# A decoder kernel: silus ahead of the second gates, projection at the tenth scan state, and the halves of a rotation ahead of its sum of squares

## The chip, the cores and the metric

The kernel runs on one core of a Trainium2 chip. TensorE (PE) multiplies matrices into PSUM, VectorE (DVE) and ScalarE (ACT) do the elementwise work and reductions, GpSimd (POOL) does elementwise work on SBUF alone, and SyncE (SP) issues transfers. Each engine takes its instructions in order; semaphores hold one until another engine's result is there or a buffer is free. The metric is the device time of one execution in microseconds (us), as the median of several runs.

## The reference

Two decoder layers work on x of shape (4, 512, 128), all in float32. Layer 0 is a selective state-space block, a cross attention and a mixture of experts; layer 1 is a banded attention, a cross attention, and a small transformer of two sublayers with local attention. The change touches the first and the last of these. Cut to what matters:

```python
# layer 0: selective scan, d_inner = 256, 16 states
x_part, z = split(rmsnorm(x) @ in_proj.T)
u = silu(causal_conv(x_part) + conv_b)
dt, Bm, Cm = split(u @ x_proj_w.T)
delta = softplus(dt @ dt_proj_w.T + dt_proj_b)
h[t] = exp(delta[t] * A) * h[t-1] + delta[t] * Bm[t] * u[t]   # for each of 16 states
y[t] = sum over states of h[t] * Cm[t], plus u[t] * D
out = (y * silu(z)) @ out_proj_w.T + x
```

```python
# layer 1, local attention: 8 heads of 64, windows of 64, twice
q, k, v = split(shift_token(x) @ wqkv)
q = q / clip(norm(q), 1e-12) * q_scale      # k likewise
q = q * cos * scale + rotate_half(q) * sin * scale   # k with 1 / scale
o = softmax over the own and the preceding window, times v
x = x + o @ wo;  x = x + feed_forward(layernorm(shift_token(x)))   # gated by gelu
```

## The kernel before, in words

Two stages matter. In both, the order of the instructions on every engine is written out by hand (`manual_schedule`): each helper issues its instructions when it is called, and each engine keeps that order.

**The scan** (pool "m2ps"). It steps through 4 batches of 16 states, `steps[k] = (b, n)`. One state holds two chunks of 128 channels side by side in tiles of 128x1024. Per state, ACT makes the decays `dA` (`decay`, L438, three states ahead), PE spreads the rows of B and C over the partitions (`rows`: pb and pc, two states ahead; ACT copies pc to cb, L433), DVE multiplies pb by du and scans (`scan`, L443 and L446), POOL multiplies h by cb (L451), and PE adds h to y (`collect`). pb has two PSUM buffers; pc has one, y one of two banks, h three buffers in SBUF. Beside each batch runs the preparation of the next (the table `ahead`, by state n): convolution, `gates_next` at n = 4 and 5 (PE product into a bank, ACT copy into sz, and at n = 5 the silus), `double_next` at 6 (product of u, two ACT copies), `steps_next` at 7 and 8, `parts` at 9, `corrected` and `reduced` at 10, `logarithms` and `deltas` at 11, `deltas` and `products` at 12 and 13. The preceding batch is finished beside it too: `gated` at n = 1, `projected` at 11 (16 matmuls into a bank po), `summed` at 12 (DVE reads po, L479, then the statistics, with `ve` at L179 and a POOL power), `normed4` at 14. A list `aside` gives one step of the weights' preparation for the cross attention (`blocks`, `g_part`, `v_part`) at n = 9, 10, 13 and 14; four steps each fall to batches 0, 1 and 2, the rest to n = 0 to 7 of batch 3. All of these products (gates, double, steps, projected, aside) share one PSUM bank, tag "po": a new one waits until the one before has been read for the last time.

**The local attention** (pool "la"). It goes through 32 row tiles i (two sublayers of four batches of four), each in two halves p with four heads, `g = 2 i + p`. For one g, the loop issues `scores(g+1)` (PE psc, DVE row maxima nm), `weights(g)` (PE transposes ptp, ACT copy pT), `exponentials(g+1)` (ACT), `values(g-1)` (PE pa, DVE rc and at), and around them, from the table `around`, the preparation of tiles ahead: `project_qk` of tile i+3 with `squares` (PE pqk, one PSUM buffer of two banks; ACT squares into sq, L1460), at p = 1 `rotated_a`, `norms` and `rotated_b` of tile i+3, and `turn_k`, `turn_q` of tile i+1 (PE ptk and ptq), `project_v`, `turn_out` and `output` (PE po, DVE xa, L1589). These PE results rotate through three PSUM buffers of tag "pt". The table `feed` spreads the feed-forward network over the tiles of the following batch: its gates (`ff_gates`) take pqk's buffer for two of their three products, in the tiles i = 7, 11, .. 27.

The rotation of one tile is: `rotated_a`, DVE multiplies pqk by the cosine table into ta (L1473); `norms`, DVE sums sq by head into ss (L1466) and bounds it from below (L1467); `halves`, DVE multiplies the swapped halves of pqk by the sine table into tb (L1480, two instructions, the last readers of pqk); `halves_added`, POOL adds tb to ta (L1486); `lengths`, POOL raises ss to the power -0.5 into rn (L157); `scaled`, POOL multiplies ta by rn (L1494). sq and tb share one buffer, so halves come behind the sum and the next squares behind POOL's addition. The first three tiles are prepared beside the preceding stage by the table `first`, with the calls in the order norms, rotated_a, halves, halves_added, and lengths and scaled later.

Of the kernel before, what the change touches and what calls it, by code (L numbers as in the profile page):

```python
# [11 lines left out]
F32 = mybir.dt.float32  # L12
BF16 = mybir.dt.bfloat16
I32 = mybir.dt.int32
AF = mybir.ActivationFunctionType
ALU = mybir.AluOpType
# [3 lines left out]
P = 128  # L20
# [37 lines left out]
def decoder_kernel(ctx: ExitStack, tc: tile.TileContext, a: dict):  # L58
    nc = tc.nc
    V, S, G, TE = nc.vector, nc.scalar, nc.gpsimd, nc.tensor  # L60


    cp = ctx.enter_context(tc.tile_pool(name="const", bufs=1))
# [44 lines left out]
    G.memset(cminus, -1.0)  # L108
    eps = cp.tile([P, 1], F32, tag="eps", name="eps")
    G.memset(eps, 1e-5)  # L110


    hm16 = cp.tile([P, 16], F32, tag="hm16", name="hm16")
# [123 lines left out]
    with ExitStack() as ph:  # L237
# [8 lines left out]
        u = bp.tile([P, 2, B, T], F32, tag="u", name="u")  # L246
        sz = bp.tile([P, 2, B, T], F32, tag="sz", name="sz")
# [31 lines left out]
        def unit(b):  # L279
            xns[b] = fp.tile([P, NJ, D], F32, tag="e", name="xn")  # L280
            for j in range(NJ):
                S.activation(xns[b][:, j, :], x0[:, b * NJ + j, :], AF.Identity, scale=inv[:, b, j:j + 1])
# [12 lines left out]
        def gates(b, c, pi):  # L295
            mm(pi, w_in[:, (2 + c) * P:(3 + c) * P], xnp[:, 3:])
# [64 lines left out]
        with tc.tile_pool(name="m1ps", bufs=1, space=PSUM) as ps, tc.manual_schedule():  # L361
# [9 lines left out]
            pi = ps.tile([P, T], F32, tag="pi1", name="pi")  # L371
# [5 lines left out]
            pi = ps.tile([P, T], F32, tag="pi0", name="pi")  # L377
# [36 lines left out]
        with tc.tile_pool(name="m2", bufs=3) as t2, \  # L414
# [9 lines left out]
            def rows(k):  # L424

                b, n = steps[k]
                pbs[k] = ps.tile([P, 2, T], F32, tag="pb", name="pb", bufs=2)
                for c in range(2):
                    mm(pbs[k][:, c, :], sel[:, n, :], stk[:, b, :])
                pc = ps.tile([P, T], F32, tag="pc", name="pc")  # L430
                mm(pc, sel[:, NST + n, :], stk[:, b, :])
                cbs[k] = t2.tile([P, T], F32, tag="cb", name="cb")
                S.copy(cbs[k], pc)  # L433

            def decay(k):
                b, n = steps[k]
                for c in range(2) if k else (1, 0):
                    S.activation(dAs[k % 4][:, c, c:T], delta[b % 2][:, c, c:T], AF.Exp,  # L438
                                 scale=negA[:, c * NST + n:c * NST + n + 1])

            def scan(k):
                pb = pbs.pop(k)
                V.tensor_tensor(pb, du[steps[k][0] % 2], pb, ALU.mult)  # L443
                h = hcs[k] = t2.tile([P, 2, T], F32, tag="h", name="h")
                cs = [slice(0, 2)] if k + 1 < len(steps) else [slice(0, 1), slice(1, 2)]
                V.tensor_tensor_scan(h.rearrange("p c t -> p (c t)"), dAs[k % 4].rearrange("p c t -> p (c t)"),  # L446
                                     pb.rearrange("p c t -> p (c t)"), 0.0, ALU.mult, ALU.add)
                cb = cbs.pop(k)
                for c in cs:
                    n = c.stop - c.start  # L450
                    G.tensor_tensor(h[:, c], h[:, c], cb.unsqueeze(1).to_broadcast([P, n, T]), ALU.mult)  # L451

            def collect(k):
                b, n = steps[k]
                if n == 0:
                    ys[b] = ps.tile([P, 2, T], F32, tag="y", name="y")
                hc = hcs.pop(k)
                for c in range(2):
                    mm(ys[b][:, c, :], ident, hc[:, c, :], start=n == 0, stop=n == NST - 1)

            def gated(b):
                y = ys.pop(b)
                ygs[b] = t2.tile([P, 2, T], F32, tag="yg", name="yg", bufs=1)
                for c in range(2):
                    V.scalar_tensor_tensor(ygs[b][:, c, :], u[:, c, b, :], vcol("Dp", c), y[:, c, :],
                                           ALU.mult, ALU.add)
                    (V if b == B - 1 else G).tensor_tensor(ygs[b][:, c, :], ygs[b][:, c, :], sz[:, c, b, :], ALU.mult)
# [71 lines left out]
            def bank():  # L539
                return ps.tile([P, T], F32, tag="po", name="pi")  # L540


            def turn_next(b):
                by_features(b, bank().rearrange("p (j t) -> p j t", t=P))
# [8 lines left out]
            def gates_next(b, c):  # L553
                pi = bank()
                gates(b, c, pi)
                S.copy(sz[:, c, b, :], pi)
                if c:
                    for t, i in ((u, b), (sz, b)) + ((sz, 0),) * (b == 1):
                        S.activation(t[:, :, i, :], t[:, :, i, :], AF.Silu)

            def double_next(b):
                double(b, bank()[0:104])
# [11 lines left out]
            with tc.manual_schedule():  # L574
                for k in range(3):
                    decay(k)
                for k in range(2):
                    rows(k)
                unit(1)
                turn_next(1)  # L580
                n_ = len(steps)
                for k in range(n_):
                    scan(k)
                    b, n = steps[k]
                    if k + 3 < n_:
                        decay(k + 3)
                    if k + 2 < n_:
                        rows(k + 2)
                    if n == 1 and b:
                        gated(b - 1)  # L590
                    if k:
                        collect(k - 1)
                    if b + 1 < B:
                        for f, *c in ahead.get(n, []):
                            f(b + 1, *c)
                    if n > 13 and b + 2 < B:
                        {14: unit, 15: turn_next}[n](b + 2)
                    if b and n in (11, 12, 14):
                        {11: projected, 12: summed, 14: normed4}[n](b - 1)
                    if b == B - 1 and n in (12, 13, 15):  # L600
                        {12: first_norm, 13: first_unit, 15: first_turn}[n]()
                    if aside and (n in (9, 10, 13, 14) or b == B - 1 and n < 11):
                        f, of = aside.pop(0)
                        f(of)
                assert not aside
                collect(n_ - 1)
                gated(B - 1)
                for f in (projected, summed, normed4):
                    f(B - 1)
# [372 lines left out]
    with tc.tile_pool(name="xa", bufs=3) as t1:  # L982
# [129 lines left out]
        for k in range(NT + 3):  # L1112
            for half, tile_ in enumerate((tile_a, tile_b)):
                with tc.manual_schedule():
# [3 lines left out]
                    n = 2 * k + half - 25  # L1118
# [300 lines left out]
    with tc.tile_pool(name="la_b", bufs=2) as bp, tc.tile_pool(name="la_t", bufs=2) as t1, \  # L1419
# [14 lines left out]
        hTs, pqks, tas, tbs, rns, sss, qTs, pes, pTs, ats, aTs = ({} for _ in range(11))  # L1434
# [28 lines left out]
        def norms(i):  # L1463

            ss = sm.tile([P, 16], F32, tag="ss16", name="ss16")
            V.tensor_reduce(ss, sss.pop(i).rearrange("p w h d -> p (w h) d"), AX.X, ALU.add)  # L1466
            V.tensor_scalar_max(ss, ss, 1e-24)  # L1467
            sss[i] = ss

        def rotated_a(i):  # L1470
# [3 lines left out]

        def halves(i):
            src = pqks.pop(i).rearrange("p w (h d) -> p w h d", d=64)
            tb = tbs[i] = t1.tile([P, 2, 8, 64], F32, tag="sq", name="tb", bufs=1)
            for hf in range(2):
                lo = slice(32 * hf, 32 * hf + 32)
                V.tensor_tensor(  # L1480
                    tb[:, :, :, lo], src[:, :, :, 32 - 32 * hf:64 - 32 * hf],
                    tabs[i // NT][:, i % NJ, 1, :, lo].unsqueeze(2).to_broadcast([P, 2, 8, 32]), ALU.mult)
# [11 lines left out]
            G.tensor_tensor(ta, ta, rns.pop(i).unsqueeze(2).to_broadcast([P, 16, 64]), ALU.mult)  # L1494

        def rotated_b(i):
            for f in (halves, halves_added, lengths, scaled):
                f(i)

        def turn_q(i):  # L1500
# [291 lines left out]
        def x_norm(b):  # L1792
            normal(x5[:, b * NJ:(b + 1) * NJ, :], *mvs.pop(("x", b)))


        first = {9: [(shift, 0)], 10: [(project_qk, 0), (squares, 0)],
                 11: [(norms, 0), (rotated_a, 0), (halves, 0), (halves_added, 0)],
                 12: [(project_qk, 1), (squares, 1), (lengths, 0)],
                 13: [(project_v, 0), (norms, 1), (rotated_a, 1), (halves, 1), (scaled, 0)],
                 14: [(halves_added, 1), (project_qk, 2), (squares, 2)], 15: [(lengths, 1), (turn_k, 0), (turn_q, 0)],  # L1800
                 16: [(project_v, 1), (norms, 2), (rotated_a, 2), (halves, 2), (scaled, 1)],
                 17: [(halves_added, 2)], 18: [(lengths, 2), (scores, 0)], 19: [(scaled, 2), (exponentials, 0)]}


        around = [[[], [(turn_k, 1), (turn_q, 1)], [(project_qk, 3), (squares, 3)]],
                  [[(turn_out, -1), (rotated_a, 3)], [(norms, 3), (rotated_b, 3)], [(project_v, 2), (output, -1)]]]

        feed = {(0, 0): [[], [], [(ff_hidden, 2, 0)]], (0, 1): [[], [(ff_hidden, 2, 1)], []],
                (1, 0): [[(ff_shift, 1)], [(ff_hidden, 2, 2)], []],
# [14 lines left out]
        with tc.manual_schedule():  # L1824
# [25 lines left out]
            for g in range(last):  # L1850
                i, p = divmod(g, 2)
# [183 lines left out]
```

## Time and profile before

| what | value |
|---|---|
| median of 3 runs | 1233.97 us (1232.23 to 1235.54) |
| the profiled execution: its own time | 1233.73 us |
| its span | 1231.7 us |
| granted TensorE clock, mean | 0.957 |
| busy, PE / DVE / ACT / POOL | 88 / 73 / 59 / 52% of the span |
| the scan | about 36 to 310 us |
| local attention with its prologue | about 805 us to the end |

The span is the time from the first to the last instruction of the profiled execution; its own time holds 2.0 us more. A line of a timeline gives the start (us), the duration (us), the engine, the line of the kernel, the operation, what it writes and reads with shapes, and in brackets the idle time of the engine ahead of it and what ended that. A line of waits gives the engine and line that waited, what it waited for, and the total, the number and the longest of these waits. "PEld" is TensorE's loading of weights; ptq and other names are tiles, without their buffer numbers.

### The profile page before, as it was taken

To read this page: it belongs to the slowest core of one execution; us is meant where nothing else is said; L and a number is where in the kernel's file an instruction comes from. 1 tells how busy PE (TensorE), PEld (TensorE's weight loads), DVE (VectorE), ACT (ScalarE), POOL (GpSimd) and SP (SyncE) were. 2 spreads that over 40 slices of the span, in tenths; PEclk is the share of its full clock that TensorE was granted. 3 is DMA by queue.
4 is the path that set the end of the run, shared out by engine and by line. 5 is a ranking of instruction groups with operands and counts; after the bars stand their busy time and mean duration, and the time that the engine had idled before them with its cause. 6 is when DMAs were issued, how large, how long until landed. Compare 5 with 4: busy or idle time off the path is not lost.

```text
span 1231.7 us, 22149 instructions
## 1 busy us (share of the span) xinstructions
PE 1081.4 (88%) x8377; PEld 698.5 (57%) x8377; DVE 895.8 (73%) x1691; ACT 731.2 (59%) x1629; POOL 644.7 (52%) x554
## 2 busy tenths in 40 slices
PE   5879879787778889989999998787999999999995
PEld 2324333443456679966666665455666566666564
DVE  5878888898668274867867676787777676676753
ACT  5696867764364454546566665246665765766762
POOL 5458586776454432644201111367786576576641
PEclk9799989898799899999999999899999999999998
DMA  9000000000400342300000000000110110011100
GB/s 280 1 0 1 0 1 1 0 1 0 154 1 14 137 154 76 85 27 25 2 2 2 2 2 2 0 9 19 32 28 18 28 27 18 22 24 28 27 20 28
DMA packets 38739, 39.96 MB, mean 32 GB/s; under 512 B 7544, under 2 KB 29833, under 8 KB 38153
## 3 DMA queue, kind: packets, MB, share of 16 engines
q1 hardware_dynamic: 36041, 32.73, 9.2%
q0 software_dynamic: 2048, 4.20, 1.2%
q10 hardware_dynamic: 544, 1.62, 0.5%
q8 instruction: 66, 1.08, 0.4%
q14 instruction: 40, 0.33, 0.1%
HBM read 20.80 MB, written 9.18 MB: 24 GB/s over the span
## 4 chain that ended last, share of the span: by engine, by line
PE 46%; DVE 18%; ACT 4%; issue 2%; POOL 2%; DMA 1%; DVEq 0%; ACTq 0%; POOLq 0%; SPq 0%
PE psc L189 9%; PE pa L189 4%; PE pqk L189 4%; PE ptp L1287 4%; PE po L189 3%; PE pff L189 3%; PE phg L189 3%; PE pog L189 3%; DVE tb L1480 2%; PE pv L189 2%; DVE ss L1466 2%; DVE ta L1473 2%; PE pof L189 2%; PE pq L189 1%; DMA hn<-xa 1%
## 5 line engine op out<-in xcount | busy, mean ns | idle before, releaser
L451 POOL TENSOR_TENSOR h<-h,cb 128x1024 f32<-128x1024 f32 (+1 forms) x65 | 151.8, 2337 | 72.0 <-DVE h L446 59.8
L157 POOL TENSOR_TENSOR rs<-ve,cneg 128x1 f32<-128x1 f32 (+2 forms) x74 | 56.1, 758 | 210.9 <-DVE ve L166 175.7
L446 DVE TENSOR_TENSOR_SCAN h<-dA,pb 128x1024 f32<-128x1024 f32 x64 | 146.3, 2286 | 21.7 <-PE y L189 7.4
L1277 ACT ACTIVATE pe<-psc,nm 128x256 f32<-128x256 f32 (+1 forms) x256 | 93.4, 448 | 69.7 <-DVE nm L1270 68.9
L189 PE MATMUL y<-h,ident 128*128 128x512 f32 x256 | 128.9, 628 | 6.1 <-POOL h L451 5.4
L1486 POOL TENSOR_TENSOR ta<-ta,tb 128x1024 f32<-128x1024 f32 x32 | 75.4, 2356 | 102.5 <-DVE rc L1570 56.2
L1270 DVE TENSOR_REDUCE nm<-psc 128x4 f32<-128x1024 f32 (+1 forms) x64 | 69.8, 1090 | 43.1 <-PE psc L189 37.9
L157 POOL TENSOR_TENSOR rn<-ss,cneg 128x16 f32<-128x16 f32 x32 | 93.0, 2906 | 0.0
L1540 DVE TENSOR_REDUCE nm<-psc 128x4 f32<-128x512 f32 x64 | 44.0, 687 | 63.8 <-PE psc L189 62.0
L438 ACT ACTIVATE dA<-delta,negA 128x511 f32<-128x511 f32 (+1 forms) x128 | 85.3, 715 | 6.3 <-POOL delta L352 4.4
L189 PEld LDWEIGHTS y<-h,ident 128*128 128x128 f32 x256 | 49.7, 198 | 67.5 <-issue 47.2
L940 ACT ACTIVATE hTg<-phg,bias 128x128 f32<-128x128 f32 x184 | 52.3, 368 | 46.6 <-PE phg L189 45.0
L443 DVE TENSOR_TENSOR pb<-du,pb 128x1024 f32<-128x1024 f32 x64 | 77.5, 1211 | 2.4 <-POOL du L355 1.5
L1549 ACT ACTIVATE pe<-psc,nm 128x128 f32<-128x128 f32 x256 | 73.6, 380 | 5.0 <-DVE nm L1540 4.9
L189 PE MATMUL pqk<-f_qkv,hT 128*128 128x512 f32 x128 | 65.0, 631 | 4.1 <-DVE tb L1480 4.1
L1287 PE MATMUL ptp<-ident,pe 128*128 128x128 f32 x448 | 64.9, 282 | 4.0 <-ACT pT L1289 2.0
L189 PE MATMUL psc<-kb,qk 64*128 64x256 f32 (+1 forms) x512 | 66.4, 378 | 0.0
L189 PE MATMUL pb<-stk,sel 96*128 96x512 bf16 x128 | 41.2, 405 | 25.9 <-DVE h L446 15.5
L1494 POOL TENSOR_TENSOR ta<-ta,rn 128x1024 f32<-128x1024 f32 x32 | 60.8, 1901 | 2.4
L1287 PEld LDWEIGHTS ptp<-ident,pe 128*128 128x128 f32 x448 | 48.7, 141 | 20.4 <-ACT pT L1289 7.8
L1460 ACT ACTIVATE sq<-pqk 128x1024 f32<-128x1024 f32 x32 | 32.9, 1029 | 43.6 <-PE pqk L189 40.3
L189 PE MATMUL pff<-hnT,f_w 128*128 128x512 f32 (+3 forms) x108 | 48.7, 571 | 9.6 <-DVE tb L1480 7.3
(391 smaller groups left out, 2810.1 us busy)
## 6 DMA issues: line engine op xcount, KB each, us to landing
vh<-va SPq DMA_DIRECT2D x56, 130.0 KB
w<-in_e_w_dram SPq DMA_DIRECT2D x16, 256.0 KB
xs<-zero SPq DMA_DIRECT2D x2, 1472.0 KB
xg<-xs SPq DMA_DIRECT2D x10, 256.0 KB
ys<-yg SPq DMA_DIRECT2D x10, 256.0 KB
f_qkv<-in_f_qkv_dram SPq DMA_DIRECT2D x1, 1536.0 KB
x<-in_x_dram SPq DMA_DIRECT2D x4, 256.0 KB
w_kv<-in_w_kv_dram SPq DMA_DIRECT2D x1, 1024.0 KB
```

Of the source, the lines that this page charges most:

```text
L157: G.tensor_tensor(out, in_, cneg.to_broadcast([P, n]), ALU.pow)
L189: TE.matmul(out, lhsT=lhsT, rhs=rhs, start=start, stop=stop)
L438: S.activation(dAs[k % 4][:, c, c:T], delta[b % 2][:, c, c:T], AF.Exp, scale=negA[:, c * NST + n:c * NST + n + 1])
L443: V.tensor_tensor(pb, du[steps[k][0] % 2], pb, ALU.mult)
L446: V.tensor_tensor_scan(h.rearrange("p c t -> p (c t)"), dAs[k % 4].rearrange("p c t -> p (c t)"), pb.rearrange("p c t -> p (c t)"), 0.0, A ...
L451: G.tensor_tensor(h[:, c], h[:, c], cb.unsqueeze(1).to_broadcast([P, n, T]), ALU.mult)
L1270: V.tensor_reduce(nm, psc[:, :, 0:nk], AX.X, ALU.max, negate=True)
L1277: S.activation(pe[:, h, 0:nk], psc[:, h, 0:nk], AF.Exp, bias=nm[:, h:h + 1])
L1287: TE.transpose(ptp[:, h * nb + kk, :], pe[:, 2 * pr + h, kk * P:(kk + 1) * P], ident)
L1486: G.tensor_tensor(ta, ta, tbs.pop(i).rearrange("p w h d -> p (w h) d"), ALU.add)
L1494: G.tensor_tensor(ta, ta, rns.pop(i).unsqueeze(2).to_broadcast([P, 16, 64]), ALU.mult)
L1549: S.activation(pes[g][:, h, :], o[:, par, q, :], AF.Exp, bias=nm[:, k:k + 1])
```

## The change

It has four parts. In `gates_next` the second call no longer copies its product into sz: the silus of u and of the first half of sz are issued first, and the last silu reads the product in PSUM and writes sz. `projected` moves from state 11 to state 10. The lower bound of the sum of squares becomes a `tensor_tensor` maximum against a column `least` of 1e-24, which is filled at the start, instead of a `tensor_scalar` maximum. In the loop of local attention `norms` moves behind `halves` and `halves_added`, and tb has a buffer of its own. The table `first` is as it was.

```diff
+    least = cp.tile([P, 1], F32, tag="least", name="least")
+    G.memset(least, 1e-24)
...
             def gates_next(b, c):
                 pi = bank()
                 gates(b, c, pi)
-                S.copy(sz[:, c, b, :], pi)
-                if c:
-                    for t, i in ((u, b), (sz, b)) + ((sz, 0),) * (b == 1):
-                        S.activation(t[:, :, i, :], t[:, :, i, :], AF.Silu)
+                if not c:
+                    S.copy(sz[:, c, b, :], pi)
+                    return
+                S.activation(u[:, :, b, :], u[:, :, b, :], AF.Silu)
+                S.activation(sz[:, 0, b, :], sz[:, 0, b, :], AF.Silu)
+                if b == 1:
+                    S.activation(sz[:, :, 0, :], sz[:, :, 0, :], AF.Silu)
+                S.activation(sz[:, c, b, :], pi, AF.Silu)
...
-                    if b and n in (11, 12, 14):
-                        {11: projected, 12: summed, 14: normed4}[n](b - 1)
+                    if b and n in (10, 12, 14):
+                        {10: projected, 12: summed, 14: normed4}[n](b - 1)
...
-            V.tensor_scalar_max(ss, ss, 1e-24)
+            V.tensor_tensor(ss, ss, least.to_broadcast([P, 16]), ALU.max)
...
-            tb = tbs[i] = t1.tile([P, 2, 8, 64], F32, tag="sq", name="tb", bufs=1)
+            tb = tbs[i] = t1.tile([P, 2, 8, 64], F32, tag="tb", name="tb", bufs=1)
...
-            for f in (halves, halves_added, lengths, scaled):
+            for f in (halves, halves_added, norms, lengths, scaled):
...
-                  [[(turn_out, -1), (rotated_a, 3)], [(norms, 3), (rotated_b, 3)], [(project_v, 2), (output, -1)]]]
+                  [[(turn_out, -1), (rotated_a, 3)], [(rotated_b, 3)], [(project_v, 2), (output, -1)]]]
```

## The prediction

> **What bounds the kernel now.** Three views, in this order: the page (busy shares), the waits of the local-attention loop (870 to 1185 us), and the timelines of one tile of it and of one batch of the scan.
>
> The page says no more than that TensorE is the fullest engine:
>
> ```profile
> PE 1081.4 (88%) x8377; PEld 698.5 (57%) x8377; DVE 895.8 (73%) x1691; ACT 731.2 (59%) x1629; POOL 644.7 (52%) x554
> ```
>
> By stage it splits. The table of windows gives PE 45.60 busy of 47.40 us per batch of local attention (96%, clock 1.00): a stall of PE there is nearly all paid. In the scan (40 to 310 us) the pace is DVE's, 3.54 us a state (1.34 for the product, 2.20 for the scan). The waits of the local loop (total, times, longest):
>
> ```profile
> PE pff L189 <- DVE tb L1480: 7.3, 6, 1.2
> ...
> PEld ptq L1504 <- DVE xa L1589: 4.4, 14, 1.0
> ```
>
> The first is what the change aims at: six times PE waits 1.2 us until `halves` frees pqk. The second matters more. Fourteen times the queries' transpose waits for `xa`, the last small work of DVE in a tile, since ptq takes the "pt" bank that `xa` reads. Most of these waits are about 0.3 us: DVE reaches `xa` just late already, so any time added to DVE between `ta` and `xa` is PE's. One such tile:
>
> ```profile
> 953.67 1.21 DVE L1473 TENSOR_TENSOR ta<-pqk,tab 128x1024 f32<-128x1024 f32 x1
> ...
> 954.80 1.21 DVE L1466 TENSOR_REDUCE ss<-sq 128x16 f32<-128x1024 f32 x1
> ...
> 956.04 0.17 DVE L1467 TENSOR_SCALAR ss<-ss 128x16 f32<-128x16 f32 x1
> 956.12 1.28 DVE L1480 TENSOR_TENSOR tb<-pqk,tab 128x512 f32<-128x512 f32 x2
> ...
> 957.32 0.17 DVE L1570 RECIPROCAL rc<-pa 128x4 f32<-128x4 f32 x1
> ...
> 957.55 2.37 POOL L1486 TENSOR_TENSOR ta<-ta,tb 128x1024 f32<-128x1024 f32 x1 [3.10 <-DVE rc L1570]
> ...
> 957.87 0.28 DVE L1589 TENSOR_TENSOR xa<-po,x 128x128 f32<-128x128 f32 x1
> ...
> 958.20 0.42 PEld L1504 LDWEIGHTS ptq<-ident,ta 128*128 128x128 f32 x4 [0.25 <-DVE xa L1589]
> ```
>
> `ta` gives way at 954.80, `rc` starts at 957.32: 2.52 us (sum 1.24, bound 0.08, halves 1.20). POOL starts 0.23 us behind `rc`'s start.
>
> **Local part: halves first.** pqk comes free 1.32 us sooner. Behind it sits PE only in the six tiles with the feed-forward gates (i = 7, 11, .. 27). There PE waits 1.22 us (the matmul itself); the weight wait is 1.41. With halves at 964.64 and done by 965.9, PE arrives at 966.1 and waits no more: 6 x 1.22 = -7.3 us. The second buffer for tb also removes the one wait of `sq` on POOL (3.3 us at 831.5, in the prologue); POOL is busy almost without a gap from 828 to 847 and the next pox waits 0.90 us on DVE, so I take -0.8 (0 to -2.9).
>
> **Local part: the bound.** The new order starts POOL's addition (2.36 us) while DVE sums (1.14 us, `sq` alone), and then puts a tensor_tensor of two SBUF tensors on DVE while POOL still adds. The same form (a small tile against a broadcast column) stands in the trace beside the same POOL instruction:
>
> ```profile
> 814.49 2.34 POOL L1486 TENSOR_TENSOR ta<-ta,tb 128x1024 f32<-128x1024 f32 x1 [2.65 <-DVE tb L1480]
> ...
> 816.05 0.80 DVE L179 TENSOR_TENSOR ve<-mv,eps 128x4 f32<-128x4 f32 x1
> ```
>
> `ve` costs 0.16 us as a median; here it ends at 816.85 with POOL's 816.83. At 855.51 it ends with POOL again, at 159.41 and 229.44 it lasts 2.02 and 2.01 beside POOL's h. The old form is no better off: L1467's one long case (0.92 instead of 0.17, at 898.79) ends with POOL's xab at 899.67. Here a rule of the Trainium skill can be weighed. "VectorE: DVE Perf Modes" (section "Why `tensor_tensor` can't do 2×_2P or 4×") says an fp32 tensor_tensor has no two-port mode; read alone, it would make the column form a way around POOL, cost 0.17 and the local part -8.1. "SBUF — State Buffer" ("Who interferes with whom") says that a DVE instruction with two SBUF inputs contends with a GpSimd instruction that reads SBUF, and the one behind waits for the whole of the other. The four rows above are of the second kind; I take it. Below nothing this cannot go: the bound cannot end before the sum.
>
> So: from the end of halves, POOL starts at +0.23 and runs 2.36; DVE's next work starts 0.06 before POOL's end (816.77 against 816.83): +2.53. It was sum and bound, 1.32. Each tile's `rc`, `at`, `xa` come 1.2 us later. Queued behind the waiting bound are these, in tiles i = 4, 8, .. also `ge` (whose bank the next ptp takes); for them wait ptp or ptq on PE, and the ACT copies of qT and hn. `lengths` waits for the bound too, but POOL had over 2 us free.
>
> 29 tiles run this order (i = 0 to 28). In the six with gates DVE is idle 2.94 us afterwards, so nothing is lost. In the other 23 the delay meets PE: 14 shown waiting for xa, seven with `ge` ahead of it, i = 0, where DVE leads the chain (it is in the chain of waits from 848.98 to 855.71), and i = 3. 23 x 1.2 = +27.6. If only the 15 or so with a shown wait count: +18. Local sum: 27.6 - 7.3 - 0.8 = **+19.5 us**.
>
> **Scan: silus ahead of the second gates.** ACT in scan batch 1:
>
> ```profile
> 128.81 0.57 ACT L433 COPY cb<-pc 128x512 f32<-128x512 f32 x1
> 130.32 0.58 ACT L556 COPY sz<-pi 128x512 f32<-128x512 f32 x1 [0.94 <-PE pi L189]
> 130.92 1.28 ACT L559 ACT_TABLE_LOAD   x1
> 132.22 1.06 ACT L559 ACTIVATE u<-u 128x1024 f32<-128x1024 f32 x1
> 133.18 1.04 ACT L559 ACTIVATE sz<-sz 128x1024 f32<-128x1024 f32 x1
> 134.22 1.28 ACT L438 ACT_TABLE_LOAD   x1
> 135.52 1.33 ACT L438 ACTIVATE dA<-delta,negA 128x512 f32<-128x512 f32 x2
> ```
>
> The wait of 0.94 and the copy of 0.58 go; the table load can start at 129.3. Two silus of 512 (about 0.58 each, by the copies of that size) replace one of 1.04: +0.1. Net 1.5 us sooner for dA at 135.52, then cb, pc, collect and the scan at 139.67, which waits 2.44. The bank is held until the last silu, so the next projection starts at about 132.8 instead of 133.3: no loss. 1.5 us in batches 1 and 2. In batch 0 PE waits 2.60 us for the same cb and then runs y in 3.43 us instead of 1.88 (granted clock 0.57 from 70 to 74); after 1.65 us idle, in batches 1 and 2, it doesn't. The wait shrinks below 1.65, so this 1.6 goes too: -3.1. Together -6.1 (from -4.5, if the clock stays low, to -6.1).
>
> **Scan: projection a state earlier.** DVE's `x` waits for po: 2.11, 2.11 and 0.86 us in batches 1 to 3. These waits go. But in batches 1 and 2 the tenth state also takes a side step (pk, pv) in the same single bank, and its matmuls now come behind po and ahead of `summed`. PE is then parked from about 152.6 until `summed` has read po, two scans later (155.5). Behind it queue the next rows and collects, on ACT the side copies, dA and the logarithms; `deltas` on POOL waits for those. Worked through for batch 1: logarithms 4 us later, POOL's rs at about 168.3 instead of 164.8, `mr` on DVE waits for it, scan 15 at 169.9 instead of 169.99. The 2.11 and the 1.86 that `ve` spends behind POOL are given back: 0. In batch 2 the step is pv (1.95 instead of 0.61): +0.7. Ends: -4 each if nothing is given back, +2 each if the parked PE falls to the low clock for longer (TensorE's granted clock is 0.54 after its 5.1 us idle at 160). Batch 3 has no side step: -0.9. Sum -0.2; scan **-6.3 us**.
>
> The `least` memset is one POOL memset of 0.10 us behind eps, with DVE and PE waiting for x's load: 0. Nothing that is moved issues a DMA, and no SP queue is passed.
>
> **Sum.** 1231.7 + 19.5 - 6.3 = 1244.9 of span; 2.0 us lie around it (1233.73 less 1231.7): 1246.9. That run stands 0.2 below the median 1233.97, so I say **1247**.
>
> **Rivals.**
> 1. The bound isn't held by POOL (0.12). Then local is -8.1, scan -6.3: 1233.7 - 14.4 = 1219. For it: a POOL power (rn, 903.36 to 906.26) runs and `ve` at 903.87 takes 0.16. Against: that one reads 16 columns; beside the large addition, it held each time. This ends on the other side: with the bound under about 0.7 us in the 23 tiles (14.4 / 23 = 0.63 of delay) the change gains.
> 2. The delay counts only where the trace shows xa waited for (0.13): 15 x 1.2 - 8.1 - 6.3 = +3.6: 1237.
> 3. More waits (0.20): `ve` of the feed-forward norm, now beside POOL's scaled (1.90), and PE parked at the low clock: up to 7 x 1 + 2 x 1.5 = +10: about 1254.
> 4. As summed (0.55): 1242 to 1251.
>
> A time within 0.3% (3.7 us) is about what a measurement can't tell from no change. Slower: 0.55 + 0.20 + half of case 2 (0.06) = 0.81; within: 0.07; faster: 0.12. The range leaves out case 1 and the top of case 3: 1235 to 1256.
>
> **What would show it.** Right: L1467 at some 1.4 us in the median, ending with POOL's addition; ptq waiting 1.2 us or more for xa; no pff wait for tb; dA behind the silus 1.5 us sooner; a side step's PE waiting for `x` in scan batches 1 and 2; PE's share in local attention falling to 92 or 93%. Wrong: L1467 still near 0.17, or long with ptq no later, which would say that the tie of xa is looser than read.

## The result, and the profile after

The changed kernel takes 1254.19 us (1250.41 to 1256.08, 4 runs), the kernel before 1233.78 beside it: a ratio of 1.0163 (95%: 1.0147 to 1.0179), +20.4 us. The forecast was 1247 (1235 to 1256). The profiled execution after spans 1252.5 us, 20.8 more than before.

On the page, VectorE's busy time has grown by 38 us (from 895.8), and nothing else has moved much:

```profile
PE 1088.7 (87%) x8377; PEld 705.6 (56%) x8377; DVE 933.7 (75%) x1691; ACT 731.5 (58%) x1629; POOL 646.1 (52%) x555
```

The group of the bound says where. Its columns are the number, the busy time in us, the mean in ns and the idle time ahead; the window is the local attention with its prologue. First before, then after:

```profile
L1467 DVE TENSOR_SCALAR ss<-ss 128x16 f32<-128x16 f32 x32 | 6.5, 202 | 1.1
L1473 DVE TENSOR_TENSOR ss<-ss,least 128x16 f32<-128x16 f32 x32 | 42.6, 1331 | 1.1
```

The difference is 36.1 us, nearly all of VectorE's growth. One tile of the local loop, first VectorE, then POOL, then TensorE:

```profile
963.04 1.28 DVE L1486 TENSOR_TENSOR tb<-pqk,tab 128x512 f32<-128x512 f32 x2
964.24 1.21 DVE L1472 TENSOR_REDUCE ss<-sq 128x16 f32<-128x1024 f32 x1
965.48 1.38 DVE L1473 TENSOR_TENSOR ss<-ss,least 128x16 f32<-128x16 f32 x1
966.78 0.17 DVE L1576 RECIPROCAL rc<-pa 128x4 f32<-128x4 f32 x1
966.98 0.42 DVE L1577 TENSOR_TENSOR at<-pa,rc 128x256 f32<-128x256 f32 x1
967.33 0.28 DVE L1595 TENSOR_TENSOR xa<-po,x 128x128 f32<-128x128 f32 x1
```

```profile
964.46 2.36 POOL L1492 TENSOR_TENSOR ta<-ta,tb 128x1024 f32<-128x1024 f32 x1 [4.15 <-DVE tb L1486]
```

```profile
967.66 0.66 PE L1510 MATMUL ptq<-ident,ta 128*128 128x128 f32 x4 [1.22 <-DVE xa L1595]
```

The bound starts at 965.48 beside POOL's addition and ends at 966.86, with the addition (966.82). So it does in all 29 tiles of the new order: it ends 0.03 to 0.04 us after POOL's addition. rc, at and xa follow, and TensorE has stood 1.22 us for xa. In the waits of the local loop (870 to 1200 us) `pff <- tb` is gone, and TensorE's waits for xa have grown (the PEld line was 4.4 us in 14 waits). First the matmul's own wait before, then three lines after:

```profile
PE ptq L1504 <- DVE xa L1589: 0.8, 1, 0.8
```

```profile
PEld ptq L1510 <- DVE xa L1595: 22.3, 20, 1.7
...
PE ptq L1510 <- DVE xa L1595: 17.4, 14, 1.5
...
PEld ptk L1519 <- POOL ta L1492: 7.8, 7, 1.8
```

By stretches of the two profiled executions the 20.8 us are: start-up -1.3, scan (first to last scan) -4.5, the stages between the last scan and the first local tile +2.3, prologue (`ta` of tile 0 to tile 3) +3.1, loop (`ta` of tile 3 to tile 31) +17.9, tail +3.4.

### The profile page after: what moved, and what is told of

It is laid out like the page before. It is cut to its first block, busy times and chain, and to the rows that moved or that the text cites. A ratio compares the mean times of both kernels' runs of the same rounds, so it can differ in the third digit from the quotient of the medians.

```text
span 1252.5 us, 22150 instructions
## 1 busy us (share of the span) xinstructions
PE 1088.7 (87%) x8377; PEld 705.6 (56%) x8377; DVE 933.7 (75%) x1691; ACT 731.5 (58%) x1629; POOL 646.1 (52%) x555
## 4 chain that ended last, share of the span: by engine, by line
PE 44%; DVE 23%; ACT 4%; issue 3%; POOL 2%; DMA 0%; DVEq 0%; ACTq 0%; POOLq 0%; SPq 0%
PE psc L191 9%; PE pqk L191 4%; PE pa L191 4%; PE ptp L1293 4%; PE po L191 3%; DVE ss L1473 3%; PE pff L191 3%; PE phg L191 3%; PE pog L191 3%; DVE tb L1486 2%; DVE ss L1472 2%; DVE ta L1479 2%; PE pof L191 2%; DVE nm L1546 1%; PE pq L191 1%
## 5 line engine op out<-in xcount | busy, mean ns | idle before, releaser
L191 PE MATMUL phg<-xgT,wt 128*128 128x128 f32 x368 | 50.9, 282 | 4.8 <-DVE wt L938 4.5
```

Source lines behind the costliest of these rows:

```text
L191: TE.matmul(out, lhsT=lhsT, rhs=rhs, start=start, stop=stop)
```

## The experiments

Two stretches are read in every trace, from the starts of the scans and of `ta`: the local loop, which repeats to 0.6 us between kernels with the same code in it, and the scan by batch, which repeats to 2 (268.1 to 269.9 us from first to last scan in four kernels without its edits, 265.3 to 267.2 in five with both). Each kernel is compared with the kernel before on the same chip. For e5, e6, e8 and e9 that took 1250.6 us, for e12 1248.8, so ratios are compared, not times. The code below is cut; the kernels hold the rest of each edit.

### The two stages alone

e1 is the kernel before with the scan's two edits, e2 with the local ones:

```diff
 e1
...
+                S.activation(sz[:, c, b, :], pi, AF.Silu)
...
+                        {10: projected, 12: summed, 14: normed4}[n](b - 1)
 e2
...
+            V.tensor_tensor(ss, ss, least.to_broadcast([P, 16]), ALU.max)
...
+            tb = tbs[i] = t1.tile([P, 2, 8, 64], F32, tag="tb", name="tb", bufs=1)
...
+            for f in (halves, halves_added, norms, lengths, scaled):
...
```

> The kernel before with the two scan edits alone (silus ahead of the second gates, projection at the tenth state). Theory (the local bound is the whole loss, the scan gains): the changed kernel's trace has the end of the scan 5.8 us earlier, 4.5 of it since the first scan, so 1233.8 - 4.5 to 5.8 = 1228 to 1229. Rival (the scan's gain is lost again in the stages behind it, where the changed kernel's trace gives back 2.3 us before the first local tile): 1231 to 1234.

> The kernel before with the local edits alone (halves first, own buffer for tb, bound from a column). Theory: the changed kernel less the scan's gain, 1254.2 + 4.5 to 5.8 = 1259 to 1260. Rival (part of the +20 is the scan's, by TensorE being parked): 1247 to 1254, the prediction's local sum of +19.5 at the lower part.

e1: 1232.57 us, 0.9985 (0.9969 to 1.0001). e2: 1252.38, 1.0142 (1.0115 to 1.0169). Both fell in the rivals' ranges, though the rivals' reasons do not show: e1 has the scan's gain in its trace (265.46 us from first to last scan, before 269.87), and from the last scan to the first local tile it takes 508.0 us, before 508.5. What its trace gives back is in the prologue (39.67 us instead of 37.59), which it does not touch. The loss is the local part's; how much of the scan's 4.4 us reaches the end is not shown by e1, whose interval ends at -3.8.

### The bound: out of the way, or in its old form

e3 adds the 1e-24 on POOL ahead of the power; e4 has the old instruction in the new order:

```diff
 e3
-            V.tensor_tensor(ss, ss, least.to_broadcast([P, 16]), ALU.max)
...
-            rpow(rns[i], sss.pop(i), 16)
+            ss = sss.pop(i)
+            G.tensor_tensor(ss, ss, least.to_broadcast([P, 16]), ALU.add)
+            rpow(rns[i], ss, 16)
 e4
-            V.tensor_tensor(ss, ss, least.to_broadcast([P, 16]), ALU.max)
+            V.tensor_scalar_max(ss, ss, 1e-24)
```

> The changed kernel, but the bound leaves VectorE: the lower bound is added to the sum of squares on POOL just ahead of its power (0.2 us there), so no small VectorE instruction meets POOL's addition. (The bound is an addition of 1e-24 instead of a maximum with it.) Theory (the bound held behind the addition costs 1.2 us in 23 tiles, and 1.76 once in the prologue): 1254.2 - 27.6 - 1.8 = 1224.8, with the other gains of the change left. Rival (the order itself delays VectorE, e.g. its sum or the reciprocals beside POOL's addition): 1247 to 1254, and another small instruction is long in the bound's place.

> The changed kernel, with the old form of the bound (a maximum with a constant, one tensor input) in the new order. Theory (the order puts it beside POOL's addition, and either form is held there, as the old form's one long case of 0.92 us suggests): about 1254, the bound 1.3 to 1.4 us long. Rival (only the form with two tensor inputs is held): the bound stays at 0.17 and the time comes to about 1225, as without the bound.

e3: 1218.62 us, 0.9861 (0.9831 to 0.9892). One move of a 128x16 step turns the loss into a gain, 6 us more than expected. Some 4.8 of these are the bound's own time: without it the spacings of the tiles without gates are 0.1 to 0.3 us shorter than before (two differ: 0.0 and 0.9), so here VectorE's work ahead of xa counts in both directions. Its timeline of VectorE, and POOL's in the same tile:

```profile
950.24 1.21 DVE L1472 TENSOR_REDUCE ss<-sq 128x16 f32<-128x1024 f32 x1
951.37 0.17 DVE L1577 RECIPROCAL rc<-pa 128x4 f32<-128x4 f32 x1
951.58 0.42 DVE L1578 TENSOR_TENSOR at<-pa,rc 128x256 f32<-128x256 f32 x1
951.92 0.28 DVE L1596 TENSOR_TENSOR xa<-po,x 128x128 f32<-128x128 f32 x1
```

```profile
950.47 2.38 POOL L1491 TENSOR_TENSOR ta<-ta,tb 128x1024 f32<-128x1024 f32 x1 [2.70 <-DVE tb L1485]
952.80 0.22 POOL L1496 TENSOR_TENSOR ss<-ss,least 128x16 f32<-128x16 f32 x1
```

rc, at and xa run beside POOL's addition at their usual lengths (they read PSUM), and so does the sum, which has one input in SBUF: only the bound was held.

e4: 1249.41 us, 1.0115 (1.0086 to 1.0145): the form does not matter. The old form, 0.17 us in the kernel before, is held as long:

```profile
962.90 1.21 DVE L1472 TENSOR_REDUCE ss<-sq 128x16 f32<-128x1024 f32 x1
964.14 1.38 DVE L1473 TENSOR_SCALAR ss<-ss 128x16 f32<-128x16 f32 x1
965.44 0.17 DVE L1576 RECIPROCAL rc<-pa 128x4 f32<-128x4 f32 x1
```

The local loop says it without the noise of the rest (us from `ta` of tile 3 to `ta` of tile 31, and the prologue ahead of it):

| kernel | loop | prologue |
|---|---|---|
| before | 317.63 | 37.59 |
| scan edits only: e1, e5, e6 | 317.66, 317.69, 317.68 | 39.67, 40.42, 37.61 |
| e7 (column, old order) | 317.86 | 39.62 |
| changed | 335.49 | 40.65 |
| e2, e4 | 334.95, 335.32 | 39.06, 39.33 |
| e10 (addition in two) | 311.18 | 38.66 |
| e3, e8, e9, e11 (bound on POOL) | 304.88, 304.90, 304.89, 304.82 | 39.43, 39.17, 39.16, 39.35 |

### The form in the old place, and how long the hold lasts

```diff
 e7 (the kernel before)
...
-            V.tensor_scalar_max(ss, ss, 1e-24)
+            V.tensor_tensor(ss, ss, least.to_broadcast([P, 16]), ALU.max)
 e10 (the changed kernel)
-            G.tensor_tensor(ta, ta, tbs.pop(i).rearrange("p w h d -> p (w h) d"), ALU.add)
+            tb = tbs.pop(i).rearrange("p w h d -> p (w h) d")
+            for k in (slice(0, 8), slice(8, 16)):
+                G.tensor_tensor(ta[:, k], ta[:, k], tb[:, k], ALU.add)
```

> The kernel before with the bound from a column alone, in the old order (sum and bound ahead of the halves). Theory (only the place beside POOL's addition matters, not the form): no change, 1233 to 1235, the bound at 0.17 in nearly all tiles. Rival (two tensor inputs cost VectorE something of their own): the bound longer in most tiles and 1238 or more.

> The changed kernel, with POOL's addition of 1024 elements in two of 512 (some 1.2 us each). Theory (the bound waits for the end of the POOL instruction that runs when it comes, not for POOL to fall idle): VectorE's sum ends as the first half does, so the bound waits 0.1 to 0.3 instead of 1.2; 22 tiles x 1.1 = 24 us less than the changed kernel, a ratio to the kernel before of 0.995 to 1.0. Rival (VectorE stays out as long as POOL has additions in a row): the bound at 1.3 to 1.4 as before, ratio 1.016.

e7: 1233.63 us, 1.0007 (0.9992 to 1.0022): no change, its bound at 0.23 us in the mean. e10: 1224.09 us, 0.9928 (0.9900 to 0.9955). The same work on POOL in two instructions, and most of the hold is gone (the two of POOL stand in one line):

```profile
949.60 1.21 DVE L1472 TENSOR_REDUCE ss<-sq 128x16 f32<-128x1024 f32 x1
950.84 0.29 DVE L1473 TENSOR_TENSOR ss<-ss,least 128x16 f32<-128x16 f32 x1
951.06 0.17 DVE L1578 RECIPROCAL rc<-pa 128x4 f32<-128x4 f32 x1
```

```profile
949.83 2.51 POOL L1494 TENSOR_TENSOR ta<-ta,tb 128x512 f32<-128x512 f32 x2 [3.08 <-DVE tb L1486]
```

The bound ends at 951.13, where POOL's first half does: each half takes 1.28 us, so the first ends at 951.11. In all 29 tiles it ends 0.03 to 0.04 us after the first half. So the hold lasts to the end of the POOL instruction that runs when the bound comes. This agrees with the Trainium skill, "SBUF — State Buffer" (section "Who interferes with whom"): whoever issues first has the shared ports for its whole instruction, and one-tensor VectorE forms such as `tensor_scalar` can use them too.

### The scan, edit by edit

e5 is the kernel before with the silus alone, e6 with the projection alone; e8 is e3 with the projection back at state 11, e9 is e3 without both scan edits.

```diff
 e5
...
+                S.activation(sz[:, c, b, :], pi, AF.Silu)
 e6
-                        {11: projected, 12: summed, 14: normed4}[n](b - 1)
+                        {10: projected, 12: summed, 14: normed4}[n](b - 1)
 e8 (against e3)
-                        {10: projected, 12: summed, 14: normed4}[n](b - 1)
+                        {11: projected, 12: summed, 14: normed4}[n](b - 1)
 e9 (against e8)
...
-                S.activation(sz[:, c, b, :], pi, AF.Silu)
+                S.copy(sz[:, c, b, :], pi)
...
```

> The kernel before with the silus ahead of the second gates alone. Theory (the silus carry the scan's gain of some 4 us from first to last scan, and it reaches the end): 1229 to 1230.5. Rival (the gain is lost on the way to the end, since both scan edits together measured only -1.0): 1232.5 to 1234.

> The kernel before with the projection at the tenth state alone. Theory (TensorE, parked behind the side step until summed has read the projection, gives back the three waits that go): 0 to +2 us, 1233.5 to 1235.5. Rival (the waits of x for the projection, 5.1 us in all, are gained): 1229 to 1231.

> The changed kernel with the bound on POOL (1218.6 there) and the projection back at the eleventh state; the silus stay ahead. Theory (the early projection costs 0 to 2): 1217 to 1218.5. Rival (the early projection gains): 1219 to 1221.

> The kernel before with the local edits and the bound on POOL, without either scan edit. Theory (the scan edits are worth the 3.7 us that the traces show from the first scan to the end of the scan): 1218.6 + 3.7 = 1222.3. Rival (they are worth nothing at the end, as the pair of -1.0 alone and +1.8 on top of the local edits says): 1217 to 1219.

Ratios: e5 0.9924 (0.9895 to 0.9953), e6 1.0023 (1.0003 to 1.0044), e8 0.9848 (0.9825 to 0.9871), e9 0.9907 (0.9882 to 0.9932). On a kernel before of 1233.5 us these would be 1224.1, 1236.3, 1214.8 and 1222.0. Only e5 is clearly outside its ranges, below them; e6 (0.8 above) and e8 (2.2 below) reach theirs with their intervals, and e9 is as expected. The starts of the scans by batch (us):

| kernel | batch 0 | batch 1 | batch 2 | batch 3 to its last scan | sum |
|---|---|---|---|---|---|
| before | 70.25 | 69.66 | 70.04 | 59.92 | 269.87 |
| e9, no scan edit | 68.56 | 69.46 | 70.19 | 59.92 | 268.14 |
| e5, silus | 65.94 | 68.01 | 69.15 | 59.89 | 262.99 |
| e8, silus | 65.94 | 68.01 | 69.14 | 59.89 | 262.98 |
| e6, projection | 70.30 | 71.50 | 72.80 | 58.98 | 273.58 |
| changed (both) | 65.76 | 69.76 | 70.95 | 58.91 | 265.38 |
| e3, both | 65.57 | 69.75 | 71.05 | 58.92 | 265.29 |
| e11 (side step first) | 66.05 | 68.92 | 66.80 | 58.98 | 260.75 |
| e12 (mr on POOL) | 65.95 | 68.01 | 67.76 | 59.75 | 261.47 |

The silus gain 6.9 us (5.2 in e8 against e9), the projection loses: +2.4 on top of the silus (265.38 less 262.99; +2.3 in e3 against e8), +3.7 alone, and the ratios go the same way (e5 and e8 down, e6 up). ScalarE in batch 1 of the changed kernel: no copy ahead of the table load, and the last silu reads PSUM:

```profile
122.81 0.57 ACT L435 COPY cb<-pc 128x512 f32<-128x512 f32 x1
123.40 1.28 ACT L561 ACT_TABLE_LOAD   x1
124.70 1.06 ACT L561 ACTIVATE u<-u 128x1024 f32<-128x1024 f32 x1
125.66 0.61 ACT L562 ACTIVATE sz<-sz 128x512 f32<-128x512 f32 x1
126.18 0.58 ACT L565 ACTIVATE sz<-pi 128x512 f32<-128x512 f32 x1
```

From the end of cb's copy to dA it is 4.7 us (123.38 to 128.07); before, 6.1 (129.38 to 135.52). The bill of the early projection is TensorE behind the side step, and VectorE later behind POOL. In batch 1, the three steps of VectorE before, then TensorE and VectorE in the changed kernel:

```profile
156.97 0.69 DVE L479 SCALAR_TENSOR_TENSOR x<-x,po 128x512 f32<-128x512 f32 x1 [2.11 <-PE po L189]
...
159.41 2.02 DVE L179 TENSOR_TENSOR ve<-mv,eps 128x4 f32<-128x4 f32 x1
...
168.45 0.27 DVE L207 SCALAR_TENSOR_TENSOR mr<-mv,rs 128x4 f32<-128x4 f32 x1
```

```profile
148.05 0.71 PE L191 MATMUL pk<-ctxT,w_kv 128*128 128x128 f32 x4 [2.72 <-DVE x L481]
```

```profile
149.76 0.68 DVE L181 TENSOR_TENSOR ve<-mv,eps 128x4 f32<-128x4 f32 x1
...
160.74 2.31 DVE L209 SCALAR_TENSOR_TENSOR mr<-mv,rs 128x4 f32<-128x4 f32 x1 [3.20 <-POOL rs L159]
164.32 2.29 DVE L448 TENSOR_TENSOR_SCAN h<-dA,pb 128x1024 f32<-128x1024 f32 x1
```

x no longer waits, ve is held 0.68 instead of 2.02, but mr waits 3.20 for rs and then runs 2.31 instead of 0.27.

e11 takes e3 and issues the side step ahead of the projection; e12 moves mr of this norm to POOL:

```diff
 e11 (against e3)
+                    if aside and (n in (9, 10, 13, 14) or b == B - 1 and n < 11):
+                        f, of = aside.pop(0)
+                        f(of)
                     if b and n in (10, 12, 14):
                         {10: projected, 12: summed, 14: normed4}[n](b - 1)
...
-                    if aside and (n in (9, 10, 13, 14) or b == B - 1 and n < 11):
-                        f, of = aside.pop(0)
-                        f(of)
 e12 (against e11)
-                mvs[b] = stats4(rs_[b])
+                mv, rs = stats4(rs_[b])
+                mvs[b] = mv, rs, None, shifts(mv, rs)
```

> The changed kernel with the bound on POOL, and in the scan the side step issued ahead of the projection in the same state (so that its matmuls don't wait behind po for summed). Theory (the parked TensorE is what gave back the early projection's gain, 5.3 and some 4.5 us late in batches 1 and 2): from the first to the last scan 258 to 261 instead of 265.3 (263.0 without the early projection), and a ratio of 0.980 to 0.983, where 0.9861 stands for this kernel with the projection ahead and 0.9848 with it at the eleventh state. Rival (what is given back hangs on something else, e.g. VectorE's second scan beside the small work): 265, ratio 0.986.

> The kernel with the bound on POOL and the side step first (ratio 0.9808), with mr of the scan's norm (the mean by the inverse deviation) moved from VectorE to POOL right behind rs, as two POOL steps of 0.2 us. Theory (what is left of the parked TensorE's bill is mr, which waits 1.33 and 0.71 us for rs and is then held 2.30 us behind POOL's h instead of 0.27): the waits and the holds of batches 1 and 2 go, some 6 us less, first to last scan 254 to 256 instead of 260.75, ratio 0.975 to 0.977. Rival (the next scan waits for POOL or ScalarE there just the same, since delta and du come late): 259 to 261, ratio 0.980 to 0.982.

e11: 1210.93 us, 0.9808 (0.9789 to 0.9827), the fastest of all: no pk or pv waits for x any more, and the scan takes 260.75 us. Batch 2 gives the most (66.80 instead of 70.95), batch 1 only 0.8. e12 fell to its rival: 0.9810 (0.9759 to 0.9860), 261.47 us. mr is gone from VectorE, which in batch 1 now waits for du:

```profile
164.41 1.23 DVE L445 TENSOR_TENSOR pb<-du,pb 128x1024 f32<-128x1024 f32 x1 [1.73 <-POOL du L357]
```

Batch 1 is 0.9 us shorter than in e11, batches 2 and 3 are 1.0 and 0.8 longer, and the sum moves less than the scan repeats to. So with the side step first, mr's wait and hold cost nothing that shows in the sum: POOL's du is nearly as late. What mr costs in the changed kernel, behind the parked TensorE, was not tested alone.

## Why the prediction was right, and where it was off

**The number.** It is 7 us above the forecast's point and above the 1242 to 1251 of its own case 4. It agrees with case 3's 1254 by luck: that case's waits in the loop are not there (its `ve` takes 0.16 us), and its sum, up to +10 on 1247, would be 1257.

**The bound (+27.6 forecast).** Right in mechanism, place and size. It is held to the end of POOL's addition, 1.37 us in the median. Tile by tile, `ta` to `ta`, the changed kernel takes 1.0 to 1.5 us more than before in 21 of the 22 spacings without gates (0.47 in the other), 25.8 us in all; the last tile's bound adds 1.2 in the tail: +27.0. Case 2 (only where a wait was shown) is out: more than 15 spacings are longer. Case 1 (not held) is out by e3 against e4. What spoke for it, `ve` at its usual length beside a POOL power, holds but is about the power: in the fourteen traces `ve` falls into the power on ss 100 times and never takes more than 0.17 us. Such a pair, before:

```profile
948.04 2.90 POOL L157 TENSOR_TENSOR rn<-ss,cneg 128x16 f32<-128x16 f32 x1
```

```profile
948.56 0.16 DVE L179 TENSOR_TENSOR ve<-mv,eps 128x4 f32<-128x4 f32 x1
```

TensorE's share from 900 to 1100 us fell from 96.0 to 92.3%, as forecast.

**The gates (-7.3).** The six spacings with gates are 1.33 us shorter each: -8.0, the same in e2, e3, e4 and e10. The loop's +17.9 and the last bound make +19.1, where these two terms of the forecast make +20.3.

**Silus (-6.1).** -6.9 by e5: -4.3, -1.65 and -0.9 in batches 0, 1 and 2, where -3.1, -1.5 and -1.5 were said; -5.2 by e8 against e9. In batch 0 the spacing of the two scans where TensorE ran at the low clock shrank from 8.3 to 5.3 us, and from 8.2 to 5.3 in e8 against e9: the forecast's 3.1. Batch 0 as a whole is 2.6 us shorter there, so the rest of the -4.3 is not shown.

**Projection (-0.2).** This term was mis-sized, and its sign was wrong: +2.4 on top of the silus. The step that failed is "The 2.11 and the 1.86 that `ve` spends behind POOL are given back: 0" in batch 1, where the changed kernel is 1.75 us behind e5, and the +0.7 of batch 2, where it is 1.8. The chain was followed (parked TensorE, late logarithms, late rs, mr), but mr was taken at its usual 0.27; it comes beside POOL's h (160.67 to 163.03) and ends with it, so it took 2.31. That the 2.0 more are the 1.75 is read from the trace; e12 shows du just behind it. That the side step's place behind the projection is the cause is shown by e11 for the sum; in batch 1 alone e11 gives back 0.85 of the 1.75. Batch 3's -0.9 came out at -1.0.

**tb's own buffer (-0.8).** Not seen. The prologue is 3.1 us longer in the changed kernel, with two causes in its trace: a product psc at the low clock (2.08 us for 1.13) and one bound held 1.93 us behind `scaled`. But e5, which has no local edit, holds its bound 1.93 us there too, and the prologue differs as much between kernels with no local edit (37.6 to 40.4), so it is no measure of that term.

**What stays open.** The forecast of the deterministic parts, +13, and their measure (-4.5, +17.9, +1.2: +14.6) agree, with the scan 1.8 us worse and the local part 0.4 better than forecast. The runs say +20.4 (+18.1 to +22.1). The 5.8 between lie, in the profiled execution, in the stages between, the prologue and 2.2 us of the tail (1.5 of them at a low clock, see the end), less 1.3 at the start. e4, which differs from the changed kernel only in the bound's form, measures +14.2 (+10.6 to +17.9) where its parts give +16.2 (-2.7, +17.7, +1.2), and e3 -17.1 where its parts give -17.3. e1 is above its parts too, by 2.5 us (-1.9 by its ratio, -4.4 in its scan). The stages between took 506.0 to 511.8 us in nine kernels that have the same code there, on chips where the kernel before takes about 1233 us, so scatter of this size is there; but one execution of each kernel was profiled, and why the changed kernel is 5 us above its parts was not settled. The forecast's range held it by width, not by knowledge of this.

## What to carry to other kernels

Before moving a small VectorE instruction that works in SBUF, look at what POOL runs at its new place: beside POOL's elementwise work on 128x512 or 128x1024, the bound in both its forms, `ve` and `mr` cost what was left of POOL's instruction, though alone they take under 0.3 us, and all behind them in the queue came later too. Not every step is held: the sum, and the steps that read PSUM, ran at their usual length, and POOL's power on 128x16 held no `ve`. The ways out that were measured are to give the step to POOL, or to cut POOL's instruction in pieces. A product moved ahead in a shared bank needs a look at who takes the bank next: here the order of the two decided between a loss of 2.4 us and a gain of 2.2 from first to last scan.

## What the runs showed that was not expected

The same idle of TensorE can cost nothing or a good microsecond. In the tail TensorE waits 1.66 us in the kernel before and 1.65 after for the same `at`. First before, then after:

```profile
1192.29 0.44 PE L1578 MATMUL pto<-ident,at 128*128 128x128 f32 x2 [1.66 <-DVE at L1571]
1192.56 0.60 PE L1618 MATMUL pt<-ident,hn 128*128 128x128 f32 x4
```

```profile
1210.93 0.44 PE L1584 MATMUL pto<-ident,at 128*128 128x128 f32 x2 [1.65 <-DVE at L1577]
1211.21 0.92 PE L1624 MATMUL pt<-ident,hn 128*128 128x128 f32 x4
```

In the second, pt, the transposes and pa behind it run at the low clock, and this place costs 1.5 us. All fourteen traces have this wait, of 1.65 or 1.66 us; behind it the granted clock is 1.00 in thirteen and falls in the changed kernel's alone (0.50 from 1211.34 to 1214.75). The Trainium skill, "TensorE: Matmul & The Clock Gate" (Part 1), says that the clock is judged over a window of some 3.4 us, which runs freely and doesn't start with the kernel; the clock falls after a window of idleness. An idle of 1.65 us is half of that, so by the rule alone the clock would fall in neither. Nor does the place of the window tell the two apart: the granted clock in these traces holds for whole steps of 3.41 us (but for the last stretch of each), and the step with this wait in it has TensorE busy for 1.75 us before (1190.05 to 1193.46, counted on from its last change) and 1.76 us after (1207.93 to 1211.34). What decides in such a half-idle step stays open. It also means that the prediction's reading of the scan, where an idle of 1.65 us left the clock high, is no safe rule.
